# A sum of products moved from GpSimd to VectorE, with a PSUM copy of one operand and a buffer of its own

## The chip, the cores and the metric

The kernel runs on one core of one Trainium2 chip. The metric is device microseconds from the start to the end of one execution; the time before is the median of three runs. The engines are named as in the profile: PE is TensorE (matmul), PEld its loading of weights, DVE is VectorE, ACT is ScalarE, POOL is GpSimd, SP is SyncE, which issues most transfers.

## The reference

Two layers of a compressed interaction network, each followed by a batch norm over rows and embedding. The input has 4096 rows, 32 fields and 16 embedding values.

```python
def _cin_layer(out, x, W, b, gamma, beta):
    r, _, e = x.shape
    h = jnp.einsum('rne,rfe->rnfe', out, x).reshape(r, -1, e)
    h = jnp.einsum('rce,oc->roe', h, W) + b[None, :, None]
    return _batchnorm(h, gamma, beta)
h1 = _cin_layer(x, x, W1, b1, g1, beta1)
out, direct1 = (h1[:, :64], h1[:, 64:])
direct2 = _cin_layer(out, x, W2, b2, g2, beta2)
return jnp.concatenate([direct1, direct2], axis=1).sum(axis=-1)
```

W1 is 128 x 1024, W2 is 128 x 2048, all in 32-bit floats. Of the first layer 64 channels go on to the second, the other 64 to the output.

## The kernel before

The 65,536 sites (a row and an embedding value) stand along the free axis in tiles of 512. The **first pass** computes layer one for all of them, in 128 tiles; it is not touched by the change. Its kept channels go to memory, raw. The **second pass** computes layer two. Its loop runs over 64 **columns** c; a column is a pair of tiles, 512 sites of the one half of the rows and 512 of the other, and its matrix products are done in Strassen's way, in Winograd's form: seven products of half size in place of eight, with sums of operands made beforehand.

A column has four **stages**, k = 0 to 3, for the weight groups i = 3, 0, 1, 2 in that order. Stage 0 (i = `PLAIN`) is the **half stage**: one of its two blocks q is multiplied in the ordinary way, only q = 1 in Strassen's. Stages 1 to 3 are full. What a stage does, in the order of the code:

- ScalarE makes two factors, `f1` and `f2`: the kept channels, loaded as tile a, scaled and shifted by the batch norm. They lie in PSUM, in the pool `factors`, which has two banks.
- VectorE multiplies them with the inputs b and bx (L539): **M1**, `zz<-f,b`, makes B11 and B21, **M2**, `zz<-f,bx`, makes T3 and B22. All four stand in one tile z (named `zz`), as z[:, 0] = B11, z[:, 1] = T3, z[:, 2] = B22 and z[:, 3] = B21, each with its q; the pool of z has three tiles.
- GpSimd makes from z the **sum** T2 = T3 + B11 (L584) and the **differences** T1 = B22 - T2 and T4 = B21 - T2 in one instruction (L587), in a tile t. The pool of t has two tiles for the four stages of a column. The half stage uses one half of its tile.
- TensorE multiplies with weights of 64 output channels (L570), on one or the other half of its columns: in the half stage eight ordinary products, one of x1, two each of x32, x67 and x54; in a full stage two of x1 and four each of x32, x67 and x54. That is 15 + 3 x 14 = 57 products a column. x1 and x32 read z, x67 reads T2 and T3, x54 reads T1 and T4. The products of a stage go in the order x1, x32, then x54 of the stage before, then x67; after x67 of stage 3 stands x54 of stage 3 as well. The two halves take turns product by product, and since 57 is odd, the column that starts with the low half is followed by one that starts with the high half (`low_first`).

The sums of a column, four banks x11, x62, x34 and x57, are put together by `combine` during the next column, in steps that the main loop calls at fixed places: two copies of x11 by ScalarE, then an add by VectorE (tile `both`, stage 0), `e` = both + x62 ahead of M2 of stage 1, copies `u2` by ScalarE, `u3` behind M2 of stage 1, `e` from u3 ahead of M2 of stage 2, a reduction behind M1 of stage 3. `idle` gives some columns one more reduction, ahead of e.

Every engine runs its instructions in the order in which the code writes them: `queue` ties each to the one before on its engine.

```python
def queue(engine, make):
    with tc.issue_after(lasts[engine].ins) if engine in lasts else nullcontext():
        lasts[engine] = make()
    return lasts[engine]
```

Of the kernel before, what the change touches and what calls it, by code (L numbers as in the profile page):

```python
# [35 lines left out]
FP = mybir.dt.float32  # L36
AF = mybir.ActivationFunctionType
ALU = mybir.AluOpType
AX = mybir.AxisListType

P = 128
# [3 lines left out]
T = 512  # L45
# [16 lines left out]
def tile_cin(ctx: ExitStack, tc: tile.TileContext, xa, xb, xr, w1, w1m, w2, bn, out):  # L62
# [24 lines left out]
    class Stats:  # L87


        def __init__(self, name, tiles, groups=None):  # L90
            self.name = name
            full, rest = divmod(tiles - LAST, SG)
            self.sizes = [SG] * full + [rest] * (rest > 0) + [LAST]
            if groups is None:
                groups = const.tile([P, len(self.sizes), 3], FP, tag=f"groups{name}", name=f"groups{name}")
            self.groups = groups

            for g, size in enumerate(self.sizes):
                nc.vector.memset(groups[:, g, 0:1], size / LAST)
            self.group = self.at = 0  # L100
# [440 lines left out]
    def multiply_part(z, a, b, q):  # L541

        a = a.unsqueeze(1).to_broadcast([P, 2, T])
        dve(lambda: nc.vector.tensor_tensor(z[:, :, q], a, b.rearrange("p (k q) t -> p k q t", k=2)[:, :, q], ALU.mult))  # L544
# [10 lines left out]
    class Sums:  # L555
# [11 lines left out]
        def matmul(self, x, w, b, stop=False):  # L567
            start = x not in self.started
            self.started.add(x)
            queue("pe", lambda: nc.tensor.matmul(self.of[x], w, b, start=start, stop=stop))  # L570

    class Stage:


        def __init__(self, sums_, i, z, last):
            self.matmul, self.stop = sums_.matmul, last
            self.w = [weights(i, q) for q in range(2)]
            self.b11, self.t3, self.b22, self.b21 = (z[:, k] for k in range(4))
# [5 lines left out]
            queue("pool", lambda: nc.gpsimd.tensor_tensor(t[:, 0, q], z[:, 1, q], z[:, 0, q], ALU.add))  # L584

            twice = t[:, 0, q].unsqueeze(1).to_broadcast([P, 2, n, T])
            queue("pool", lambda: nc.gpsimd.tensor_tensor(t[:, 1:3, q], z[:, 2:4, q], twice, ALU.subtract))  # L587
# [5 lines left out]
        def ordinary(self, low_first, q):  # L593
            a11, a21, a12, a22, s1, s2, s3, s4 = self.w[q]
            minus_s3, minus_a21 = neg_sb[:, 0, q], neg_sb[:, 1, q]
            for x, u, y, v in ((3, s4, 2, a11), (5, s1, 4, a21)):
                self.two(low_first, (x, u, self.b22[:, q], False), (y, v, self.b11[:, q], False))
            for x, u, y, v in ((3, minus_s3, 2, a12), (5, minus_a21, 4, a22)):
                self.two(low_first, (x, u, self.t3[:, q], False), (y, v, self.b21[:, q], False))

        def x1(self, low_first):

            halves = [(x, self.w[q][0], self.b11[:, q], True) for x, q in zip((1, 0), self.qs)]
            if len(self.qs) == 1 and not low_first:
                halves[0] = (0, *halves[0][1:])
            self.two(low_first, *halves)

        def products(self, low_first, x, kx, bx, y, ky, by):
            for q in self.qs:
                stop = q == 1  # L610
                self.two(low_first, (x, self.w[q][kx], bx[:, q], stop), (y, self.w[q][ky], by[:, q], stop))

        def x32(self, low_first):
            self.products(low_first, 3, 7, self.b22, 2, 2, self.b21)
# [74 lines left out]
    for c in range(NC):  # L689
        raw, b, bx = loaded(c)  # L690
        sums_ = Sums()
        g = c // DIFF + 1
        if g < NC // DIFF:
            if c % DIFF == 2:
                with tc.issue_after(loads[-1].ins):
                    for k in range(2):
                        load_x(g, k)
            if c % DIFF == 4:
                for k in range(2):
                    queue("act", lambda: negate(k))  # L700
                idle += [lambda k=k: difference(k) for k in range(4)]
            if c % DIFF == 10:
                queue("act", lambda: store_difference(g))

        f1 = factor(raw[STAGES[0]], STAGES[0], 0)
        for k, i in enumerate(STAGES):

            z = z2pool.tile([P, 4, 2, T], FP, tag="zz", name="zz")
            if c == k == 0:

                f2 = factor(raw[i], i, 1)
                for q in range(2):
# [12 lines left out]
            if k == 1:  # L725
                step()
            if k < 3:
                f1 = factor(raw[STAGES[k + 1]], STAGES[k + 1], 0)
            if k == 0:
                step(2)  # L730
            if k == 2:

                step()
            for _ in range(min(len(sums_left), 4 if c == NC - 1 else 1)):
                queue("act", sums_left.pop(0))
            if k == 1:
                step()

            stage = Stage(sums_, i, z, k == 3)
# [111 lines left out]
```

## Time and profile before

| | |
|---|---|
| median of three runs | 2152.68 us (2151.9 to 2153.17) |
| the profiled execution | 2154.79 us, of which its span 2153.1 us |
| granted clock of TensorE, mean | 0.996 |
| GpSimd sum L584, full stage | 192 of 2372 ns |
| GpSimd differences L587, full stage | 192 of 4566 ns |
| GpSimd sum L584, half stage | 64 of 1288 ns |
| GpSimd differences L587, half stage | 64 of 2380 ns |
| VectorE M1 and M2 (L539) | 510 of 2.28 us |

The page counts busy time for each engine over the whole span; the first pass fills about the first 497 us and has nearly no work for GpSimd. A "wait" is idle time of an engine ahead of an instruction, put down to what ended it. The rows on which the argument rests stand in the prediction.

### The profile page before, as it was taken

What the parts mean: (1) busy time and instruction counts of PE and PEld (TensorE: products, weight loads), DVE (VectorE), ACT (ScalarE), POOL (GpSimd) and SP (SyncE); (2) the same over time, 40 slices, a digit from 0 to 9 for tenths busy, and PEclk for the clock granted to TensorE, in tenths of its full rate; (3) what the DMA queues carried; (4) which work ended last, traced back from release to release, by engine and by line L of the source; (5) the groups of instructions that cost most, each with busy time, mean ns of one, the idle gap of its engine ahead of it and who ended that gap; (6) DMA issues with size and microseconds to landing.
All of it is one profiled execution on the core that took longest, in us unless ns stands there. A gap on an engine that the chain in (4) does not pass through costs nothing.

```text
span 2153.1 us, 23463 instructions
## 1 busy us (share of the span) xinstructions
PE 2104.0 (98%) x8604; PEld 736.7 (34%) x8604; DVE 1846.4 (86%) x1317; ACT 969.0 (45%) x1522; POOL 1561.7 (73%) x519
## 2 busy tenths in 40 slices
PE   9999999999999999999999999999999999999996
PEld 3444444443333333333333333333333333333332
DVE  8898888988888888888888888888888888888885
ACT  3555555553444444444444444444444444444443
POOL 0000000006999999999999999999999999999996
PEclk9999999999999999999999999999999999999998
DMA  9999999997779777676787776676777777676751
GB/s 361 349 336 350 330 356 350 348 335 179 168 168 207 178 171 164 157 166 157 171 188 178 169 169 162 156 166 157 180 168 169 167 171 162 157 166 159 169 132 39
DMA packets 112019, 440.64 MB, mean 205 GB/s; under 512 B 13088, under 2 KB 13088, under 8 KB 103456
## 3 DMA queue, kind: packets, MB, share of 16 engines
q1 hardware_dynamic: 105456, 418.43, 73.4%
q10 hardware_dynamic: 6448, 20.72, 2.5%
q8 instruction: 67, 1.10, 0.2%
q14 instruction: 48, 0.39, 0.1%
HBM read 417.07 MB, written 22.02 MB: 204 GB/s over the span
## 4 chain that ended last, share of the span: by engine, by line
PE 44%; POOL 29%; DVE 14%; issue 12%; ACT 0%; DMA 0%; POOLq 0%; DVEq 0%; SPq 0%
PE x L570 22%; PE ps L384 21%; POOL t L587 20%; POOL t L584 9%; DVE zz L539 9%; DVE e L534 2%; DVE d L667 2%; PE ps L346 2%; ACT both L531 0%; DMA b<-in_xb 0%; DVE zz L544 0%; POOLq L847 0%; DVE xd L192 0%; PE running L412 0%; DVE u L534 0%
## 5 line engine op out<-in xcount | busy, mean ns | idle before, releaser
L587 POOL TENSOR_TENSOR t<-zz,t 128x2048 f32<-128x2048 f32 (+1 forms) x256 | 1029.0, 4020 | 20.1
L584 POOL TENSOR_TENSOR t<-zz 128x1024 f32<-128x1024 f32 (+1 forms) x256 | 537.8, 2101 | 545.1 <-DMA a<-h 493.0
L570 PE MATMUL x<-zz,s_sb 128*64 128x512 f32 x2048 | 920.4, 592 | 0.7 <-PE running L412 0.7
L570 PE MATMUL x<-zz,w_sb 128*64 128x512 f32 x2304 | 915.0, 592 | 0.0
L570 PE MATMUL x<-t,s_sb 128*64 128x512 f32 x1792 | 824.9, 594 | 12.1 <-POOL t L587 12.1
L531 ACT ACTIVATE f<-a,keep 128x512 f32<-128x512 f32 x512 | 398.0, 778 | 409.3 <-DVE zz L539 403.3
L539 DVE TENSOR_TENSOR zz<-f,b 128x2048 f32<-128x2048 f32 x255 | 581.0, 2279 | 0.0
L539 DVE TENSOR_TENSOR zz<-f,bx 128x2048 f32<-128x2048 f32 x255 | 580.6, 2277 | 0.0
L384 PE MATMUL ps<-z,w_sb 128*128 128x512 f32 x1024 | 449.9, 597 | 2.6 <-DVE z L353 2.6
L570 PE MATMUL x<-t,w_sb 128*64 128x512 f32 x896 | 429.6, 596 | 14.2 <-POOL t L587 14.1
L570 PEld LDWEIGHTS x<-zz,w_sb 128*64 128x64 f32 x2304 | 282.6, 137 | 347.2 <-issue 346.4
L570 PEld LDWEIGHTS x<-zz,s_sb 128*64 128x64 f32 x2048 | 272.2, 137 | 293.9 <-issue 289.8
L353 DVE TENSOR_TENSOR z<-a,b 128x2048 f32<-128x2048 f32 (+1 forms) x129 | 294.1, 2281 | 60.5 <-DMA b<-in_xb 36.6
L570 PEld LDWEIGHTS x<-t,s_sb 128*64 128x64 f32 x1792 | 239.9, 137 | 274.5 <-issue 224.1
L384 PEld LDWEIGHTS ps<-z,w_sb 128*128 128x128 f32 x1024 | 192.4, 190 | 257.9 <-issue 245.5
L534 DVE TENSOR_TENSOR both<-both,x 128x512 f32<-128x512 f32 x64 | 44.0, 688 | 183.2 <-ACT both L531 183.2
L310 ACT ACTIVATE e<-ps,bn_sb 128x512 f32<-128x512 f32 x127 | 87.3, 687 | 239.0 <-PE ps L384 224.0
L570 PEld LDWEIGHTS x<-t,w_sb 128*64 128x64 f32 x896 | 117.3, 137 | 154.7 <-issue 110.8
L531 ACT ACTIVATE u<-e,bn_sb 64x512 f32<-64x512 f32 x64 | 46.3, 723 | 223.9 <-DVE e L534 223.9
L531 ACT ACTIVATE both<-x 64x512 f32<-64x512 f32 x64 | 38.0, 594 | 189.4 <-PE x L570 189.4
L570 PE MATMUL x<-zz,neg_sb 128*64 128x512 f32 x256 | 120.3, 592 | 0.0
L485 ACT ACTIVATE unread<-e,center 128x512 f32<-128x512 f32 x124 | 89.6, 722 | 26.3 <-DVE e L534 24.5
(88 smaller groups left out, 884.6 us busy)
## 6 DMA issues: line engine op xcount, KB each, us to landing
a<-h SPq DMA_DIRECT2D x256, 512.0 KB, 5.3
a<-in_xa SPq DMA_DIRECT2D x128, 512.0 KB, 5.8
b<-in_xb SPq DMA_DIRECT2D x128, 512.0 KB, 6.8
b<-in_xb SPq DMA_DIRECT2D x64, 1024.0 KB, 8.0
bx<-in_xb SPq DMA_DIRECT2D x64, 512.0 KB, 7.0
bx<-x SPq DMA_DIRECT2D x64, 512.0 KB, 8.8
h<-kept ACTq DMA_DIRECT2D x64, 256.0 KB, 5.8
r<-in_xr SPq DMA_DIRECT2D x16, 512.0 KB, 8.0
```

Source lines behind the costliest of these rows:

```text
L310: nc.scalar.activation(e, ps, AF.Identity, bias=b1)
L346: nc.tensor.matmul(pss[t + k], w1_sb[rows, 4 + t % GROUP // 4, :], zr[rows, :], start=not ended, stop=ended)
L353: return nc.vector.tensor_tensor(z[:, k], a.rearrange("p (a t) -> p a t", a=2)[:, k].unsqueeze(2).to_broadcast([P, n, 2, T]), b.rearrange( ...
L384: nc.tensor.matmul(pss[t], w1_sb[:, m, :], z[:, m // 2, m % 2, :], start=(t == m == 0), stop=(t > 0 and m == 3))
L485: return nc.scalar.activation(unread, e[:, s], AF.Square, bias=center[:, s], accum_out=squares[:, s, c : c + 1])
L531: return queue("act", lambda: nc.scalar.activation(to, source, AF.Identity, **scale_bias))
L534: return dve(lambda: nc.vector.tensor_tensor(to, x, y, ALU.add))
L539: dve(lambda: nc.vector.tensor_tensor(z, a, b.rearrange("p (k q) t -> p k q t", k=2), ALU.mult))
L570: queue("pe", lambda: nc.tensor.matmul(self.of[x], w, b, start=start, stop=stop))
L584: queue("pool", lambda: nc.gpsimd.tensor_tensor(t[:, 0, q], z[:, 1, q], z[:, 0, q], ALU.add))
L587: queue("pool", lambda: nc.gpsimd.tensor_tensor(t[:, 1:3, q], z[:, 2:4, q], twice, ALU.subtract))
L667: lambda: nc.vector.tensor_reduce(d2[:, :, c, :], e.rearrange("p s (r e) -> p s r e", e=EMB), AX.X, ALU.add)
```

## The change

Three edits. The half stage's sum T2 is an add on VectorE (`sum_half`) instead of one on GpSimd. Its operand B11 comes from a copy that ScalarE writes to a bank of the pool `factors`, behind M1 of stage 0; its operand T3 comes from z. And the half stage's T2, T1 and T4 have a tile of their own, `th`, in a pool of one tile, so that the two tiles t serve the three full stages. GpSimd keeps the differences of the half stage.

```diff
+    hpool = ctx.enter_context(tc.tile_pool(name="hpool", bufs=1))
...
+    def sum_products(z):
+
+        t = tpool.tile([P, 3, 2, T], FP, tag="t", name="t")
+        queue("pool", lambda: nc.gpsimd.tensor_tensor(t[:, 0], z[:, 1], z[:, 0], ALU.add))
+
+        twice = t[:, 0].unsqueeze(1).to_broadcast([P, 2, 2, T])
+        queue("pool", lambda: nc.gpsimd.tensor_tensor(t[:, 1:3], z[:, 2:4], twice, ALU.subtract))
+        return t
+
+    def sum_half(z, b11):
+
+        t = hpool.tile([P, 3, 1, T], FP, tag="th", name="th")
+        add(t[:, 0, 0], z[:, 1, 1], b11)
+        twice = t[:, 0].to_broadcast([P, 2, T])
+        queue("pool", lambda: nc.gpsimd.tensor_tensor(t[:, 1:3, 0], z[:, 2:4, 1], twice, ALU.subtract))
+        return t
...
-        def __init__(self, sums_, i, z, last):
+        def __init__(self, sums_, i, z, last, t):
...
-            t = tpool.tile([P, 3, 2, T], FP, tag="t", name="t")
-            self.t2, self.t1, self.t4 = (t[:, k] for k in range(3))
-            q = slice(self.qs[0], 2)
-            n = len(self.qs)
-            queue("pool", lambda: nc.gpsimd.tensor_tensor(t[:, 0, q], z[:, 1, q], z[:, 0, q], ALU.add))
-
-            twice = t[:, 0, q].unsqueeze(1).to_broadcast([P, 2, n, T])
-            queue("pool", lambda: nc.gpsimd.tensor_tensor(t[:, 1:3, q], z[:, 2:4, q], twice, ALU.subtract))
+
+            self.t2, self.t1, self.t4 = ({q: t[:, k, q - self.qs[0]] for q in self.qs} for k in range(3))
...
                     multiply_part(z[:, 1:3], f2, bx, q)
+                b11 = factors.tile([P, T], FP, tag="f", name="b11")
+                act(b11, z[:, 0, 1])
             else:
                 multiply(z[:, 0::3], f1, b)
...
+                if i == PLAIN:
+                    b11 = factors.tile([P, T], FP, tag="f", name="b11")
+                    act(b11, z[:, 0, 1])
                 multiply(z[:, 1:3], f2, bx)
+            t = sum_half(z, b11) if i == PLAIN else sum_products(z)
```

The other lines of the diff follow the new form of `t` and z by q. The new lines shift the numbers: in the changed kernel the full stages' sum is L576, their differences L579, the half stage's differences L587, `add` L535, `multiply` L540, `act` L532.

On GpSimd, from the last stage of one column to the first full stage of the next (column 3; a number behind a name tells tiles apart, "waits" names the engines whose progress the instruction waits for), there stood:

```order
L584 TENSOR_TENSOR t_3170<-zz_3163 128x1024 [waits DVE_49,PE_49]
L587 TENSOR_TENSOR t_3170<-zz_3163,t_3170 128x2048 [waits Pool_49]
L584 TENSOR_TENSOR t_3221<-zz_3210 128x512 [waits DVE_49,PE_49]
L587 TENSOR_TENSOR t_3221<-zz_3210,t_3221 128x2x512 [waits Pool_49]
L584 TENSOR_TENSOR t_3253<-zz_3237 128x1024 [waits DVE_49,PE_49]
L587 TENSOR_TENSOR t_3253<-zz_3237,t_3253 128x2048 [waits Pool_49]
```

and stands now:

```order
L576 TENSOR_TENSOR t_3179<-zz_3172 128x1024 [waits DVE_49,PE_49]
L579 TENSOR_TENSOR t_3179<-zz_3172,t_3179 128x2048 [waits Pool_49]
L587 TENSOR_TENSOR th_3226<-zz_3219,th_3226 128x1024 [waits DVE_49]
L576 TENSOR_TENSOR t_3258<-zz_3248 128x1024 [waits DVE_49,PE_49]
L579 TENSOR_TENSOR t_3258<-zz_3248,t_3258 128x2048 [waits Pool_49]
```

The sum on 512 elements is gone, the differences of the half stage go to `th` and wait for VectorE, and the tiles t pass over the half stage.

On VectorE at the same place, from M2 of the last stage of one column to u3 in the next, there stood:

```order
L539 TENSOR_TENSOR zz_3163<-f_3167,bx_3055 128x2048
L539 TENSOR_TENSOR zz_3210<-f_3208,b_3191 128x2x1024
L539 TENSOR_TENSOR zz_3210<-f_3212,bx_3193 128x2048
L534 TENSOR_TENSOR both_3217<-both_3217,x11_3066 128x512
L539 TENSOR_TENSOR zz_3237<-f_3215,b_3191 128x2x1024
L534 TENSOR_TENSOR e_3239<-both_3217,x62_3067 128x512
L539 TENSOR_TENSOR zz_3237<-f_3241,bx_3193 128x2048
L534 TENSOR_TENSOR u3_3247<-u2_3243,x57_3069 128x512
```

and stands now:

```order
L540 TENSOR_TENSOR zz_3172<-f_3176,bx_3062 128x2048
L540 TENSOR_TENSOR zz_3219<-f_3217,b_3200 128x2x1024
L540 TENSOR_TENSOR zz_3219<-f_3221,bx_3202 128x2048
L535 TENSOR_TENSOR th_3226<-zz_3219,b11_3223 128x512
L535 TENSOR_TENSOR both_3231<-both_3231,x11_3073 128x512
L540 TENSOR_TENSOR zz_3248<-f_3229,b_3200 128x2x1024
L535 TENSOR_TENSOR e_3250<-both_3231,x62_3074 128x512
L540 TENSOR_TENSOR zz_3248<-f_3252,bx_3202 128x2048
```

The add `th<-zz,b11` has come in between M2 of the half stage and the add of `both`.

On ScalarE at the same place, from the factors of the half stage to u2, there stood:

```order
L531 ACTIVATE f_3208<-a_3196,keep_2781 128x512
L531 ACTIVATE f_3212<-a_3196,keep_2781 128x512
L531 ACTIVATE f_3215<-a_3198,keep_2781 128x512
L531 ACTIVATE both_3217<-x11_3066 64x512
L531 ACTIVATE both_3217<-x11_3066,bn_sb_201 64x512
L531 ACTIVATE f_3241<-a_3198,keep_2781 128x512
L531 ACTIVATE u2_3243<-e_3239,bn_sb_201 64x512
L531 ACTIVATE u2_3243<-e_3239,b2_swapped_2809 64x512
```

and stands now:

```order
L532 ACTIVATE f_3217<-a_3205,keep_2781 128x512
L532 ACTIVATE f_3221<-a_3205,keep_2781 128x512
L532 ACTIVATE b11_3223<-zz_3219 128x512
L532 ACTIVATE f_3229<-a_3207,keep_2781 128x512
L532 ACTIVATE both_3231<-x11_3073 64x512
L532 ACTIVATE both_3231<-x11_3073,bn_sb_201 64x512
L532 ACTIVATE f_3252<-a_3207,keep_2781 128x512
L532 ACTIVATE u2_3254<-e_3250,bn_sb_201 64x512
L532 ACTIVATE u2_3254<-e_3250,b2_swapped_2812 64x512
```

The copy `b11` has come in behind the second factor of the half stage. Since the pool has two banks that are taken in turn, the next factor (f_3215, now f_3229) takes the bank of that second factor; before, it took the bank of the first.

More of the change, by code (lines that the diff above doesn't have):

```diff
@@ L570, in matmul @@
             queue("pe", lambda: nc.tensor.matmul(self.of[x], w, b, start=start, stop=stop))
+    def sum_products(z):
[10 more added lines that the diff above has]
+        return t
     class Stage:
-        def __init__(self, sums_, i, z, last):
+        def __init__(self, sums_, i, z, last, t):
             self.matmul, self.stop = sums_.matmul, last
             self.w = [weights(i, q) for q in range(2)]
-            self.b11, self.t3, self.b22, self.b21 = (z[:, k] for k in range(4))
+            self.b11, self.t3, self.b22, self.b21 = ([z[:, k, q] for q in range(2)] for k in range(4))
             self.qs = (1,) if i == PLAIN else (0, 1)
-            t = tpool.tile([P, 3, 2, T], FP, tag="t", name="t")
-            self.t2, self.t1, self.t4 = (t[:, k] for k in range(3))
-            q = slice(self.qs[0], 2)
-            n = len(self.qs)
-            queue("pool", lambda: nc.gpsimd.tensor_tensor(t[:, 0, q], z[:, 1, q], z[:, 0, q], ALU.add))
-            twice = t[:, 0, q].unsqueeze(1).to_broadcast([P, 2, n, T])
-            queue("pool", lambda: nc.gpsimd.tensor_tensor(t[:, 1:3, q], z[:, 2:4, q], twice, ALU.subtract))
+            self.t2, self.t1, self.t4 = ({q: t[:, k, q - self.qs[0]] for q in self.qs} for k in range(3))
         def two(self, low_first, *halves):
@@ L596, in ordinary @@
             for x, u, y, v in ((3, s4, 2, a11), (5, s1, 4, a21)):
-                self.two(low_first, (x, u, self.b22[:, q], False), (y, v, self.b11[:, q], False))
+                self.two(low_first, (x, u, self.b22[q], False), (y, v, self.b11[q], False))
             for x, u, y, v in ((3, minus_s3, 2, a12), (5, minus_a21, 4, a22)):
-                self.two(low_first, (x, u, self.t3[:, q], False), (y, v, self.b21[:, q], False))
+                self.two(low_first, (x, u, self.t3[q], False), (y, v, self.b21[q], False))
         def x1(self, low_first):
-            halves = [(x, self.w[q][0], self.b11[:, q], True) for x, q in zip((1, 0), self.qs)]
+            halves = [(x, self.w[q][0], self.b11[q], True) for x, q in zip((1, 0), self.qs)]
             if len(self.qs) == 1 and not low_first:
@@ L610, in products @@
                 stop = q == 1
-                self.two(low_first, (x, self.w[q][kx], bx[:, q], stop), (y, self.w[q][ky], by[:, q], stop))
+                self.two(low_first, (x, self.w[q][kx], bx[q], stop), (y, self.w[q][ky], by[q], stop))
         def x32(self, low_first):
@@ L737, in tile_cin @@
                 step()
-            stage = Stage(sums_, i, z, k == 3)
+            stage = Stage(sums_, i, z, k == 3, t)
             low_first = c % 2 == 0
```

## The prediction

> **What bounds the kernel now.** I read the page first: busy shares, slices, the chain that ended last, one group. The rows of engines and slices give busy time and its tenths; a group row gives count, busy time, mean ns, idle time before it.
>
> ```profile
> PE 2104.0 (98%) x8604; PEld 736.7 (34%) x8604; DVE 1846.4 (86%) x1317; ACT 969.0 (45%) x1522; POOL 1561.7 (73%) x519
> ...
> POOL 0000000006999999999999999999999999999996
> ...
> PE 44%; POOL 29%; DVE 14%; issue 12%; ACT 0%; DMA 0%; POOLq 0%; DVEq 0%; SPq 0%
> ...
> L570 PE MATMUL x<-t,s_sb 128*64 128x512 f32 x1792 | 824.9, 594 | 12.1 <-POOL t L587 12.1
> ```
>
> GpSimd's 73% is an average over a first pass without it and a second pass where it is above 90%. The chain goes through TensorE, GpSimd and VectorE, so no engine alone sets the time. The group has 1792/64 = 28 records a column, for 14 products in the code: a product is two records. A second-pass stretch, by the view of windows (PE, PEld, DVE, ACT, POOL busy, granted clock, DMA share, GB/s):
>
> ```profile
> 1000.00:1200.00 200.00, 197.01 (x896) 64.54 (x894) 173.61 (x115) 87.22 (x135) 191.77 (x64) 1.00 0.75 173
> ```
>
> GpSimd works 191.77 of 200 us and still waits, TensorE likewise, by the waits (us, times, longest):
>
> ```profile
> PEld x L570 <- POOL t L587: 93.1, 97, 3.6
> ...
> DVE both L534 <- ACT both L531: 183.2, 64, 5.9
> ...
> POOL t L584 <- PE x L570: 51.7, 63, 0.9
> ...
> DVE e L534 <- PE x L570: 29.2, 33, 2.3
> ```
>
> GpSimd waits for TensorE once in 63 of 64 columns, and TensorE for GpSimd. That is a loop; the timeline shows it (start, duration, [idle <- releaser]):
>
> ```profile
> 1190.43 1.30 POOL L584 TENSOR_TENSOR t<-zz 128x512 f32<-128x512 f32 x1
> ...
> 1202.00 2.38 POOL L584 TENSOR_TENSOR t<-zz 128x1024 f32<-128x1024 f32 x1 [0.82 <-PE x L570]
> 1204.46 4.56 POOL L587 TENSOR_TENSOR t<-zz,t 128x2048 f32<-128x2048 f32 x1
> 1208.98 2.35 POOL L584 TENSOR_TENSOR t<-zz 128x1024 f32<-128x1024 f32 x1
> 1211.41 4.55 POOL L587 TENSOR_TENSOR t<-zz,t 128x2048 f32<-128x2048 f32 x1
> 1215.92 1.28 POOL L584 TENSOR_TENSOR t<-zz 128x512 f32<-128x512 f32 x1
> 1217.28 2.37 POOL L587 TENSOR_TENSOR t<-zz,t 128x1024 f32<-128x1024 f32 x1
> ...
> 1227.47 2.37 POOL L584 TENSOR_TENSOR t<-zz 128x1024 f32<-128x1024 f32 x1 [0.82 <-PE x L570]
> ```
>
> ```profile
> 1189.16 1.02 PE L570 MATMUL x<-t,s_sb 128*64 128x512 f32 x2
> 1190.54 0.64 PE L570 MATMUL x<-t,w_sb 128*64 128x512 f32 x1 [0.36 <-POOL t L587]
> ...
> 1201.32 0.59 PE L570 MATMUL x<-t,w_sb 128*64 128x512 f32 x1
> ...
> 1207.33 0.59 PE L570 MATMUL x<-t,w_sb 128*64 128x512 f32 x1
> ...
> 1213.77 0.59 PE L570 MATMUL x<-zz,s_sb 128*64 128x512 f32 x1
> ...
> 1214.63 1.02 PE L570 MATMUL x<-zz,s_sb 128*64 128x512 f32 x2
> 1216.01 0.64 PE L570 MATMUL x<-t,s_sb 128*64 128x512 f32 x1 [0.37 <-POOL t L587]
> ```
>
> A column lasts 1215.92 - 1190.43 = 25.49 us, by 1202.00 and 1227.47 it is 25.47: I take 25.48. **The loop**: T2 of stage 2 starts at 1202.00, when x54 of stage 0 has freed its buffer (last record 1201.32 + 0.59 = 1201.91, a lag of 0.09). GpSimd runs back to back until 1211.41 + 4.55 = 1215.96; 0.05 later, at 1216.01, TensorE gets x54 of stage 3, and 11.46 after that, at 1227.47, the next buffer is free. 13.96 + 0.05 + 11.46 = 25.47.
>
> **TensorE's floor**: from 1207.33 to 1213.77 lie 15 record steps, 0.4293 each, two records side by side on the two column halves. So 57 products of a column take 57 x 0.4293 = 24.47 us. The loop costs 25.48 - 24.47 = 1.01 us a column.
>
> **The change part by part.** *Removed from GpSimd*: the half stage's sum, 1217.28 - 1215.92 = 1.36 us a column start to start. The row has 1.28 us as the duration. (The Trainium skill, "Perfetto Trace Analysis", section "GPSIMD Engine Instruction", says to time GpSimd by start-to-start spacing and not by reported durations; the two rows agree that the two differ, by 0.08. By durations, 2.35 + 4.55 for sum and differences, loop A below would be 0.08 shorter, 24.42 us, and the floor of 24.47 would set those columns.) Alone this removal would buy nothing: T2 of stage 2 starts when x54 of stage 0 frees its buffer, however early GpSimd is there.
>
> *The own buffer* breaks that wait. The two tiles t now serve three stages, so T2 of stage 2 waits for x54 of stage 3 of the column before, long done. Late next are two loops.
>
> **Loop A, the buffer again**: T2 of stage 3 now takes the tile of stage 1 and waits for its x54, whose last record ends at 1207.33 + 0.59 = 1207.92. With the lag, 1208.01; sum and differences take 1215.96 - 1208.98 = 6.98; TensorE starts 0.05 later, at 1215.04, where an unstalled TensorE would take it at 1214.63 (the records there run without a partner). It is 0.41 late, but only once: after that the two column halves run staggered by as much, and the half due for the next x54 comes free that much later anyway. What counts is the loop's length. x54 of stage 3 to the end of x54 of stage 1 is 1207.92 - 1190.54 = 17.38, and 0.09 + 6.98 + 0.05 + 17.38 = **24.50 us**.
>
> **Loop B, VectorE's e**:
>
> ```profile
> 1190.22 0.69 DVE L534 TENSOR_TENSOR e<-both,x 128x512 f32<-128x512 f32 x1 [0.94 <-PE x L570]
> 1190.83 2.28 DVE L539 TENSOR_TENSOR zz<-f,bx 128x2048 f32<-128x2048 f32 x1
> ...
> 1204.74 2.27 DVE L539 TENSOR_TENSOR zz<-f,b 128x2048 f32<-128x2048 f32 x1
> 1206.94 2.27 DVE L539 TENSOR_TENSOR zz<-f,bx 128x2048 f32<-128x2048 f32 x1
> 1211.86 0.69 DVE L534 TENSOR_TENSOR both<-both,x 128x512 f32<-128x512 f32 x1 [2.64 <-ACT both L531]
> 1212.46 2.28 DVE L539 TENSOR_TENSOR zz<-f,b 128x2048 f32<-128x2048 f32 x1
> ...
> 1218.05 0.69 DVE L534 TENSOR_TENSOR u<-u,x 128x512 f32<-128x512 f32 x1 [0.32 <-PE x L570]
> ...
> 1231.97 2.27 DVE L539 TENSOR_TENSOR zz<-f,bx 128x2048 f32<-128x2048 f32 x1
> ```
>
> In every second column (the order of the halves alternates) e waits for the last product of x67 of stage 3, begun at 1189.16; M2 of stage 1 stands behind e and ends at 1190.83 + 2.28 = 1193.11. Then GpSimd does three full stages, 3 x 6.98 (also 1208.98 - 1202.00), with lags of 0.09 and 0.05, to the next x54 of stage 3: 3.95 + 0.09 + 20.94 + 0.05 = 25.03 us from that product. x54 itself started 0.41 after that product (loop A), so the column lasts 25.03 - 0.41 = **24.62**. The other columns have loop A's 24.50. Mean 24.56.
>
> *Added on ScalarE*: the copy of B11, between f2 of stage 0 and f1 of stage 1. The trace has no such copy; the nearest row is a factor (SBUF to PSUM, 128x512), 0.78. *Added on VectorE*: T2 behind M2 of stage 0. Nearest row: both, 0.69, with 0.60 to the next start; the far end is GpSimd's 1.36 for the same work. I take 0.60. `both` and M1 of stage 1 are queued behind it, and GpSimd's differences of stage 0 wait for it.
>
> ```profile
> 1207.05 0.78 ACT L531 ACTIVATE f<-a,keep 128x512 f32<-128x512 f32 x1 [1.42 <-DVE zz L539]
> ...
> 1210.53 0.59 ACT L531 ACTIVATE both<-x 64x512 f32<-64x512 f32 x1 [2.70 <-PE x L570]
> ```
>
> Cover: VectorE stands idle 2.64 us ahead of `both` (183.2/64 = 2.86 in the mean). In the places of this column the copy runs from 1207.05 to 1207.83 beside M2, T2 from 1209.14 (M2's start and the 2.20 from M1 to M2) to 1209.83. The copy takes a factor bank, so f1 of stage 1 must wait for M2's end (1206.94 + 2.27 = 1209.21) and ends at 1210.03, still 0.50 ahead of the ScalarE `both` at 1210.53. VectorE's own loop: from `both` to M2's end is 1231.97 + 2.27 - 1211.86 = 22.38, of which the 0.32 of u goes with the earlier x54; then f1 0.04 + 0.78 and the ScalarE part of `both`, 1211.86 - 1210.53 + 0.01 = 1.34: 24.22, under 24.47. T2, at 0.60 or at 1.36, fits beside f1 and that part (2.16). So I cost both additions at nothing; without that cover T2 would cost 0.60 x 63 = 38 us.
>
> *First column*, where VectorE feeds GpSimd:
>
> ```profile
> 501.44 1.22 DVE L544 TENSOR_TENSOR zz<-f,bx 128x1024 f32<-128x1024 f32 x1
> 502.57 2.28 DVE L539 TENSOR_TENSOR zz<-f,b 128x2048 f32<-128x2048 f32 x1
> ...
> 507.13 2.37 POOL L584 TENSOR_TENSOR t<-zz 128x1024 f32<-128x1024 f32 x1 [0.44 <-DVE zz L539]
> ...
> 523.50 4.52 POOL L587 TENSOR_TENSOR t<-zz,t 128x2048 f32<-128x2048 f32 x1
> ```
>
> f1 of stage 1 must now wait for the last part of M2, 501.44 + 1.22 = 502.66; with 0.04 + 0.78 + 0.04 M1 of stage 1 starts at 503.52 instead of 502.57. GpSimd waits for VectorE at 507.13 and then has no gap up to 523.50 + 4.52 = 528.02, so this column's x54 comes 0.95 later.
>
> **Sum.** 63 column intervals x (25.48 - 24.56) = 58.0; less 0.95: 57.0 us. The profiled execution took 2154.79 us (span 2153.1 and 1.7 around it), 2.1 above the median 2152.68: 2097.8 against it, **2095.7** against the median.
>
> **The rivals.**
>
> *VectorE sets every column.* Loop B uncredited is 25.03. If e waited for the last product in all columns, or the stagger gave nothing back, the gain would be 63 x 0.45 - 0.95 = 27.4: 2125 us. Against it: e waits for TensorE in 33 columns of 64 and not in all, and the lateness of one column is covered by the stagger in the next. Chance 0.10.
>
> *The change does not do what it says*: if T2 of stage 3 waited as long as T2 of stage 2 does, the time would stay, 2152.7. The order of instructions puts sum and differences of the half stage outside the tiles t, and loop A is 0.98 shorter, so only an unseen wait could do it: 0.03.
>
> *Slower: the new add waits for GpSimd.* Its place, 1209.14, lies beside GpSimd's sum of stage 3 (1208.98 to 1211.33), and in a quicker column beside the differences, 4.55. If VectorE could not read z while GpSimd reads, the add would be held up to 4.55, and `both` and M1 with it: 22.06 + 0.60 + 4.55 = 27.21 a column, (27.21 - 25.48) x 63 + 0.95 = 110 us more, 2263. It decides from a wait of 25.48 - 22.66 = 2.82 us.
>
> ```profile
> L534 DVE TENSOR_TENSOR both<-both,x 128x512 f32<-128x512 f32 x64 | 44.0, 688 | 183.2 <-ACT both L531 183.2
> ```
>
> Against it: 64 such adds, one input from SBUF and one from PSUM as the new one, take 688 ns in the mean, beside a GpSimd that is busy nearly always. (The Trainium skill, "SBUF — State Buffer", section "Who interferes with whom", says that a VectorE instruction with two SBUF inputs contends with a GpSimd instruction that reads SBUF, and one with at most one SBUF input does not. By that rule the add from the PSUM copy is free of it; the 688 ns agree. No run here shows an add with both inputs in SBUF beside GpSimd.) Chance 0.04.
>
> **How the numbers follow.** The forecast has 0.83. Its bounds: TensorE's floor and a first column at no cost, 63 x 1.01 = 63.6, 2089.1, or 2088 with the 0.8 us by which the fastest run lies under the median; and loop B not absorbed in every second column, (24.50 + 25.03)/2 = 24.77, 63 x 0.71 - 0.95 = 43.8, 2108.9. Twelve second-pass columns also have a reduction ahead of e, which I put at the 0.60 of VectorE's other 512-element steps; in the half of them where e has no slack that is up to 3.6 us: 2112. So 2088 to 2112, which leaves out the 0.17 of the other cases. A measurement tells 0.2%, 4.3 us, from no change. Faster: 0.83 and 0.10, 0.93; the same 0.03; slower 0.04.
>
> **What the profile after would show.** Successive half-stage differences on GpSimd 24.5 to 24.6 us apart, in turn longer and shorter; sums of stage 2 without a wait for TensorE, those of stage 3 with none or a few tenths; the wait of `both` down from 2.9 us to 1 to 2; the new add near 0.69 us and the copy near 0.78, neither waited for by GpSimd; TensorE's gap at x54 of stage 3 gone from about 1 us to a tenth. Wrong would be: columns of 25.0 with e waiting each time (first rival), a wait at x54 as before (second), an add of over 0.8 us or GpSimd waiting for it (third); GpSimd durations that grow when VectorE moves nearer; a granted clock under the 1.00 of the windows, where TensorE would lose more than all of this.

## The result and the profile after

The changed kernel takes 2099.96 us (median of 4 runs, 2099.49 to 2101.45), the kernel before, run beside it, 2152.93 us (4 runs, 2151.9 to 2156.91): a ratio of 0.9752, 95% interval 0.9735 to 0.9769. That is 53.0 us faster. The forecast was 2095.7 us, 57.0 us faster, with a range of 2088 to 2112. The profiled execution took 2099.52 us, its span is 2097.7 us.

From the page of the kernel after, the same rows as of before: busy engines, the slices of GpSimd, the chain that ended last. Behind them is the 200-us window of the second pass.

```profile
PE 2073.1 (99%) x8604; PEld 1037.5 (49%) x8604; DVE 1885.7 (90%) x1381; ACT 1007.1 (48%) x1586; POOL 1479.1 (71%) x455
...
POOL 0000000003999999999999999999999999999995
...
PE 94%; DVE 2%; DMA 2%; POOL 1%; issue 0%; ACT 0%; SPq 0%; DVEq 0%; POOLq 0%; ACTq 0%
```

```profile
1000.00:1200.00 200.00, 200.00 (x930) 108.10 (x928) 185.79 (x127) 95.34 (x148) 188.08 (x58) 1.00 0.77 178
```

GpSimd went from 519 instructions to 455 and VectorE from 1317 to 1381: the 64 sums of the half stage have moved. The chain, which was 44% TensorE and 29% GpSimd, is 94% TensorE. In the window TensorE starts 930 records where it started 896: in pairs at 0.4293 us they fill 199.6 us of the 200, where they filled 192.3.

The column is measured from one half-stage difference on GpSimd to another. These are the timeline's rows of the first, the third and the last (64th), of the kernel before; then the same of the kernel after, with two columns in between.

```profile
504.31 2.37 POOL L587 TENSOR_TENSOR t<-zz,t 128x1024 f32<-128x1024 f32 x1
...
554.85 2.38 POOL L587 TENSOR_TENSOR t<-zz,t 128x1024 f32<-128x1024 f32 x1
...
2109.11 2.38 POOL L587 TENSOR_TENSOR t<-zz,t 128x1024 f32<-128x1024 f32 x1
```

```profile
501.49 2.37 POOL L587 TENSOR_TENSOR th<-zz,th 128x1024 f32<-128x1024 f32 x1 [493.26 <-DVE th L535]
...
553.03 2.38 POOL L587 TENSOR_TENSOR th<-zz,th 128x1024 f32<-128x1024 f32 x1
...
1192.54 2.37 POOL L587 TENSOR_TENSOR th<-zz,th 128x1024 f32<-128x1024 f32 x1
1195.67 2.38 POOL L576 TENSOR_TENSOR t<-zz 128x1024 f32<-128x1024 f32 x1 [0.76 <-DVE zz L540]
...
1202.66 2.37 POOL L576 TENSOR_TENSOR t<-zz 128x1024 f32<-128x1024 f32 x1
...
1210.09 2.37 POOL L576 TENSOR_TENSOR t<-zz 128x1024 f32<-128x1024 f32 x1 [0.43 <-PE x L571]
...
1217.06 2.36 POOL L587 TENSOR_TENSOR th<-zz,th 128x1024 f32<-128x1024 f32 x1
1220.81 2.37 POOL L576 TENSOR_TENSOR t<-zz 128x1024 f32<-128x1024 f32 x1 [1.38 <-DVE zz L540]
...
1241.69 2.38 POOL L587 TENSOR_TENSOR th<-zz,th 128x1024 f32<-128x1024 f32 x1
...
2052.98 2.37 POOL L587 TENSOR_TENSOR th<-zz,th 128x1024 f32<-128x1024 f32 x1
```

Before, 61 columns took 1554.26 us, 25.480 each; after, 1499.95 us, 24.589 each. Two neighbours differ: 1217.06 - 1192.54 = 24.52 and 1241.69 - 1217.06 = 24.63. The sum of stage 2 (1202.66) no longer waits for TensorE; that of stage 3 (1210.09) does, here by 0.43, and in 26 columns of 64 by the waits below; that of stage 1 waits for VectorE's M2, by 0.76 and 1.38 in turn. The waits of the kernel after, over all columns (us in total, times, longest):

```profile
DVE both L535 <- ACT both L532: 95.6, 64, 4.9
...
POOL t L576 <- DVE zz L540: 72.3, 64, 2.1
...
PEld x L571 <- POOL t L579: 28.7, 67, 3.6
DVE e L535 <- PE x L571: 26.2, 26, 2.7
...
POOL t L576 <- PE x L571: 13.3, 26, 2.1
```

**Where the time came from.** 61 columns gained 0.890 us each, 54.3 us. The two intervals ahead of the third difference took 50.54 and take 51.54, 1.0 us lost. That leaves 53.3 between the first and the last difference, and 53.0 between the medians. (The profiled executions lie 55.3 apart: before the second pass, which the change doesn't touch, and at its end they differ by the other 2 us, and the one of before was 2.1 above its median.)

### The profile page after: what moved, and what is told of

Same layout as the page of the kernel before. It is cut to its first block, busy times and chain, and to the rows that moved or that the text cites. A ratio compares the mean times of both kernels' runs of the same rounds, so it can differ in the third digit from the quotient of the medians.

```text
span 2097.7 us, 23531 instructions
## 1 busy us (share of the span) xinstructions
PE 2073.1 (99%) x8604; PEld 1037.5 (49%) x8604; DVE 1885.7 (90%) x1381; ACT 1007.1 (48%) x1586; POOL 1479.1 (71%) x455
## 4 chain that ended last, share of the span: by engine, by line
PE 94%; DVE 2%; DMA 2%; POOL 1%; issue 0%; ACT 0%; SPq 0%; DVEq 0%; POOLq 0%; ACTq 0%
PE x L571 74%; PE ps L384 19%; PE ps L346 1%; DMA b<-in_xb 1%; DVE z L353 1%; POOL t L579 1%; DMA a<-in_xa 1%; POOL t L576 0%; DVE zz L545 0%; DVE zz L540 0%; PE running L412 0%; DVE stats L106 0%; DVE e L535 0%; DVE d L801 0%; ACT f L532 0%
## 5 line engine op out<-in xcount | busy, mean ns | idle before, releaser
L571 PE MATMUL x<-zz,s_sb 128*64 128x512 f32 x2048 | 947.2, 592 | 1.0 <-PE running L412 0.7
L571 PE MATMUL x<-zz,w_sb 128*64 128x512 f32 x2304 | 886.9, 593 | 0.0
L579 POOL TENSOR_TENSOR t<-zz,t 128x2048 f32<-128x2048 f32 x192 | 875.5, 4560 | 15.1
L571 PE MATMUL x<-t,s_sb 128*64 128x512 f32 x1536 | 699.5, 595 | 0.0
L532 ACT ACTIVATE f<-a,keep 128x512 f32<-128x512 f32 x512 | 398.0, 778 | 418.1 <-DVE zz L540 360.6
L540 DVE TENSOR_TENSOR zz<-f,b 128x2048 f32<-128x2048 f32 x255 | 580.6, 2277 | 0.1
L540 DVE TENSOR_TENSOR zz<-f,bx 128x2048 f32<-128x2048 f32 x255 | 579.9, 2274 | 0.0
L576 POOL TENSOR_TENSOR t<-zz 128x1024 f32<-128x1024 f32 x192 | 455.5, 2373 | 85.7 <-DVE zz L540 72.3
L587 POOL TENSOR_TENSOR th<-zz,th 128x1024 f32<-128x1024 f32 x64 | 152.0, 2375 | 493.3 <-DVE th L535 493.3
L571 PEld LDWEIGHTS x<-zz,w_sb 128*64 128x64 f32 x2304 | 306.3, 137 | 162.2 <-issue 70.1
L571 PE MATMUL x<-t,w_sb 128*64 128x512 f32 x768 | 364.2, 597 | 2.8 <-POOL t L579 2.7
L571 PEld LDWEIGHTS x<-t,s_sb 128*64 128x64 f32 x1536 | 207.5, 137 | 226.2 <-issue 180.0
L532 ACT ACTIVATE u<-e,bn_sb 64x512 f32<-64x512 f32 x64 | 46.2, 722 | 218.3 <-DVE e L535 218.3
L571 PE MATMUL x<-th,s_sb 128*64 128x512 f32 x256 | 130.8, 592 | 0.0
L535 DVE TENSOR_TENSOR both<-both,x 128x512 f32<-128x512 f32 x64 | 44.0, 688 | 95.6 <-ACT both L532 95.6
```

Source lines behind the costliest of these rows:

```text
L532: return queue("act", lambda: nc.scalar.activation(to, source, AF.Identity, **scale_bias))
L535: return dve(lambda: nc.vector.tensor_tensor(to, x, y, ALU.add))
L540: dve(lambda: nc.vector.tensor_tensor(z, a, b.rearrange("p (k q) t -> p k q t", k=2), ALU.mult))
L576: queue("pool", lambda: nc.gpsimd.tensor_tensor(t[:, 0], z[:, 1], z[:, 0], ALU.add))
L579: queue("pool", lambda: nc.gpsimd.tensor_tensor(t[:, 1:3], z[:, 2:4], twice, ALU.subtract))
L587: queue("pool", lambda: nc.gpsimd.tensor_tensor(t[:, 1:3, 0], z[:, 2:4, 1], twice, ALU.subtract))
```

## The experiments

The theory to test: the wait for a free tile t was the bound, so the tile of its own gives the gain and the move to VectorE gives none by itself; behind it stand loop A (the tile again, stage 1 to stage 3) and loop B (VectorE's `e`), 0.03 and 0.15 over TensorE's floor of 24.47. The rivals: the gain comes from the work that GpSimd no longer does; or VectorE sets the pace. All edits are against the changed kernel. "Column" is the mean of the 61 columns from the third to the last half-stage difference in the profile, as above. All ratios are to the kernel before, which ran beside them (medians 2152.9 to 2154.5). Some rows come from different chips, so a small difference between two rows rests on the columns as much as on the times.

| kernel | us, median (range) | ratio, 95% interval | column, us |
|---|---|---|---|
| the change, first | 2099.96 (2099.49-2101.45) | 0.9752 (0.9735-0.9769) | 24.589 |
| the change, again | 2099.08 (2098.65-2099.79) | 0.9742 (0.9726-0.9758) | 24.586 |
| own buffer only | 2098.61 (2096.27-2100.27) | 0.9743 (0.9729-0.9758) | 24.595 |
| move only | 2161.45 (2161.12-2163.63) | 1.0039 (1.0024-1.0053) | 25.587 |
| both from SBUF | 2115.12 (2113.28-2115.8) | 0.9819 (0.9805-0.9834) | 24.838 |
| x67 first | 2092.84 (2092.05-2094.74) | 0.9719 (0.9704-0.9733) | 24.510 |
| tiles apart | 2098.77 (2096.51-2098.89) | 0.9742 (0.9726-0.9758) | 24.617 |
| x67 first, tiles apart | 2090.37 (2089.6-2091.25) | 0.9707 (0.9692-0.9721) | 24.471 |
| the same, sum on GpSimd | 2096.43 (2095.59-2099.15) | 0.9733 (0.9718-0.9747) | 24.587 |
| the add four times | 2112.86 (2110.74-2114.42) | 0.981 (0.9796-0.9825) | 24.779 |
| the add six times | 2203.31 (2202.51-2224.77) | 1.0255 (1.0208-1.0301) | 26.210 |

### The own buffer without the move

```diff
-        add(t[:, 0, 0], z[:, 1, 1], b11)
+        queue("pool", lambda: nc.gpsimd.tensor_tensor(t[:, 0, 0], z[:, 1, 1], z[:, 0, 1], ALU.add))
...
-                    b11 = factors.tile([P, T], FP, tag="f", name="b11")
-                    act(b11, z[:, 0, 1])
```

> The half stage keeps its sum on GpSimd, without the copy of B11, but has the tile of its own. Theory 1 (the wait for the buffer of t closed the loop, and the own buffer is what broke it): GpSimd's work sets the column, 3 x 6.98 + 1.36 + 2.34 = 24.64 us, TensorE's floor being 24.47; so 24.64 to 24.75 a column and 2100 to 2107 us, and the changed kernel's move of the sum is worth 0 to 7 us of the 53. Theory 2 (the gain came from the load taken off GpSimd, 1.36 us a column): the column stays near 25.4, 2145 to 2153 us.

2098.61 us, a little under the 2100 to 2107 expected: the whole gain, without the move. The timeline of GpSimd in this kernel shows what holds the column now.

```profile
1213.52 1.29 POOL L585 TENSOR_TENSOR th<-zz 128x512 f32<-128x512 f32 x1
1214.89 2.38 POOL L587 TENSOR_TENSOR th<-zz,th 128x1024 f32<-128x1024 f32 x1
1217.26 2.38 POOL L576 TENSOR_TENSOR t<-zz 128x1024 f32<-128x1024 f32 x1
...
1224.23 2.40 POOL L576 TENSOR_TENSOR t<-zz 128x1024 f32<-128x1024 f32 x1
...
1231.23 2.36 POOL L576 TENSOR_TENSOR t<-zz 128x1024 f32<-128x1024 f32 x1
...
1238.17 1.28 POOL L585 TENSOR_TENSOR th<-zz 128x512 f32<-128x512 f32 x1
```

No row has a wait, and in this kernel's list of waits GpSimd has only 0.7 us behind its first instruction of the second pass: it works back to back, and its own work, 1238.17 - 1213.52 = 24.65 us, is the column. So the sum on GpSimd is not free here, it is the bound; but the changed kernel has another bound of almost the same length. That the two agree to 0.01 us in the mean is chance; the pair of experiments with both loops gone, below, takes them apart.

### The move without the own buffer

```diff
-        t = hpool.tile([P, 3, 1, T], FP, tag="th", name="th")
+        t = tpool.tile([P, 3, 2, T], FP, tag="t", name="t")[:, :, 0:1]
```

> The half stage's sum goes to VectorE with the copy of B11, but its tile comes from the two tiles t as before the change. Theory 1: the loop from x54 of stage 0 through stage 2's sum on GpSimd to x54 of stage 3 is untouched, 25.48 us a column, 2150 to 2157 us; besides, VectorE's add now waits for x54 of stage 2 of the column before, some 3 us after the place it had, with the add of both behind it. Theory 2 (the load): 2096 to 2110 us, as the changed kernel.

2161.45 us, above the 2150 to 2157 expected: slower than before by 0.4%, interval 0.24 to 0.53%. The rows are from this kernel's waits, and from its timeline of VectorE and of GpSimd.

```profile
DVE t L534 <- PE x L570: 192.0, 62, 3.9
...
POOL t L575 <- DVE zz L539: 144.8, 63, 2.9
```

```profile
1217.53 0.69 DVE L534 TENSOR_TENSOR t<-zz,b 128x512 f32<-128x512 f32 x1 [3.16 <-PE x L570]
1218.13 0.68 DVE L534 TENSOR_TENSOR both<-both,x 128x512 f32<-128x512 f32 x1
1218.73 2.28 DVE L539 TENSOR_TENSOR zz<-f,b 128x2048 f32<-128x2048 f32 x1
...
1221.53 2.28 DVE L539 TENSOR_TENSOR zz<-f,bx 128x2048 f32<-128x2048 f32 x1
```

```profile
1223.98 2.38 POOL L575 TENSOR_TENSOR t<-zz 128x1024 f32<-128x1024 f32 x1 [2.25 <-DVE zz L539]
```

The sum of stage 2 on GpSimd no longer waits for TensorE, so the loop of before is not what holds this kernel. Another wait for a tile t has taken its place: the add, now early on VectorE, takes the tile of stage 2 of the column before and waits 192.0/62 = 3.1 us for TensorE to be done with it. `both`, M1, `e` and M2 of stage 1 are queued behind it, and GpSimd, with 1.36 us less to do, waits 2.3 us a column for that M2. This and the experiment before show that the gain is the buffer's; a wait on an engine is priced by what is queued behind it there.

### No copy: both operands from SBUF

```diff
-        add(t[:, 0, 0], z[:, 1, 1], b11)
+        add(t[:, 0, 0], z[:, 1, 1], z[:, 0, 1])
...
-                    b11 = factors.tile([P, T], FP, tag="f", name="b11")
-                    act(b11, z[:, 0, 1])
```

> The changed kernel without the copy of B11: VectorE's add reads T3 and B11 both from z in SBUF, and f1 of stage 1 has its old bank again. If VectorE's second input from SBUF does not meet GpSimd's reads: an add of 0.69 us, the column at 24.59 or a little less, 2096 to 2101 us. If it does and waits for the GpSimd instruction that runs (the sum of stage 3, 1210.09 to 1212.46, where the add stood at 1211.72): an add that ends up to 0.8 us later, under the 1.4 to 1.5 us that VectorE is idle ahead of both, so still 2100 to 2103 us, but a longer add in the trace. If it waits for the sum and the differences behind it (4.57 us more): both comes some 3 us late in each column, VectorE's loop is about 27 us, 2240 to 2265 us. If GpSimd is held instead: its instructions beside the add grow by up to 0.7 us, 24.6 to 25.2 a column, 2100 to 2140 us. By the Trainium skill, SBUF - State Buffer, section Who interferes with whom, the one that issues second waits for the first.

15 us slower than the change. The first two rows are the group of the half stage's add in the changed kernel and in this one; then this kernel's timeline of GpSimd and of VectorE.

```profile
L535 DVE TENSOR_TENSOR th<-zz,b 128x512 f32<-128x512 f32 x64 | 44.0, 687 | 6.7
```

```profile
L535 DVE TENSOR_TENSOR th<-zz 128x512 f32<-128x512 f32 x64 | 90.3, 1411 | 2.2
```

```profile
1216.85 2.34 POOL L576 TENSOR_TENSOR t<-zz 128x1024 f32<-128x1024 f32 x1 [0.96 <-PE x L571]
1219.27 4.87 POOL L579 TENSOR_TENSOR t<-zz,t 128x2048 f32<-128x2048 f32 x1
```

```profile
1217.91 1.83 DVE L535 TENSOR_TENSOR th<-zz 128x512 f32<-128x512 f32 x1
1220.70 0.69 DVE L535 TENSOR_TENSOR both<-both,x 128x512 f32<-128x512 f32 x1 [0.95 <-ACT both L532]
```

The mean add takes 1411 ns instead of 687. In the rows it starts at 1217.91 inside GpSimd's sum, which ends at 1219.19, and ends at 1219.74, 0.55 after it; the differences behind the sum then take 4.87 us instead of 4.56. All 62 adds that begin inside such a sum end 0.54 to 0.56 us after it, however long they had stood, and the differences of stage 3 take 4.87 us in the mean instead of 4.55, those of the other stages as before. So the add waits for the running GpSimd instruction, and the next one, beside which the add then runs, is longer by 0.32. Two cases of the expectation came together, the waiting add and the held GpSimd. The differences of stage 3 lie in both loops, and 0.32 is near to what the column lost: it went from 24.589 to 24.838, and (24.838 - 24.589) x 62 = 15.4 us is the whole loss. This is what the copy in PSUM is worth here. (The Trainium skill, "SBUF — State Buffer", section "Who interferes with whom", says that a VectorE instruction with two SBUF inputs contends with a GpSimd instruction that reads SBUF and one with at most one SBUF input doesn't; the 1411 and the 687 ns agree with both halves of it.)

### Loop B: x67 of stage 3 ahead of x54 of stage 2

```diff
+            if k == 3:
+                stage.x67(not low_first)
...
-            stage.x67(not low_first)
+            if k < 3:
+                stage.x67(not low_first)
```

> The changed kernel with one order changed: in stage 3 x67 stands ahead of x54 of stage 2. So x62 is complete four products (1.72 us) earlier, and VectorE's e (0.94 us of waiting in every second column) should not wait. If loop B sets the longer columns: they fall from 24.66 to loop A's 24.52, the mean from 24.589 to 24.52, 4 us less, 2093 to 2097 us. If loop A or GpSimd alone sets them: no change there. In the first column TensorE's one gap of 3.27 us ahead of the last x54 becomes two shorter ones, one ahead of x67 (sum of stage 3) and one ahead of x54; if the gap's length is what lowered the granted clock to 0.57 behind it, the clock stays at 1.00 there and 1.5 us more are gained.

`e` gets its last product earlier. 2092.84 us, just under the 2093 to 2097 expected, and 24.510 a column. This kernel's waits:

```profile
POOL t L576 <- PE x L571: 44.6, 62, 1.2
...
DVE e L535 <- PE x L571: 0.9, 1, 0.9
```

VectorE's `e` now waits for TensorE once in all, 0.9 us, where it waited 26 times; every column is alike, and in 62 of 64 the sum of stage 3 waits for its tile. That is loop A alone, reckoned at 24.50. Of the 7.1 us against the change, 61 x 0.079 = 4.8 are the columns'. Another 1.7 us lie ahead of the third half-stage difference, where the granted clock of TensorE now stays at 1.00; the last section comes back to that.

### Loop A: the tile of the sum apart from that of the differences

```diff
-        t = tpool.tile([P, 3, 2, T], FP, tag="t", name="t")
+        t2 = tpool.tile([P, 2, T], FP, tag="t2", name="t2")
...
+        t14 = tpool.tile([P, 2, 2, T], FP, tag="t14", name="t14")
```

> The changed kernel with the full stages' T2 in two tiles of its own and T1 and T4 in two others, in the same space. The sum of stage 3 then waits for x67 of stage 1 only, and only its differences for x54 of stage 1: loop A shrinks from 24.50 to 17.38 + 0.09 + 4.55 + 0.05 = 22.07 us. If GpSimd's wait for the buffer (13.3 us in 26 waits) is all that is between the short columns, 24.52, and TensorE's floor of 24.47: 3 us less at most, 2096 to 2100 us, since loop B still sets every second column and the stagger of the halves already covers most of it. If loop A set both kinds of columns: 24.47 in all, 2092 us.

The sum waits for no product now, as its own tile comes free earlier. 2098.77 us: no change, the interval is that of the change run again. By the half-stage differences the two kinds of columns are 24.21 and 25.04 in the mean, where they were 24.52 and 24.66: what the one gained the other gave back. By the first record of x54 of stage 3 on TensorE they are 24.53 and 24.65, with the edit and without. So loop A alone costs nothing while loop B is there: two columns in a row have the same length together. Why the long columns give back just that much (the stagger of the halves, by the prediction's argument) was not tested apart.

### Both loops, with the sum on VectorE and on GpSimd

> x67 ahead of x54 in stage 3 and the split tiles together. With loops A and B both gone, TensorE's floor sets the column: 24.47 against 24.51 with the first alone, 2.5 us less than it, 2088 to 2092 us. If something else holds x67_first at 24.51: no difference from 2092.8.

> x67 ahead of x54 in stage 3 and the split tiles, but the half stage's sum on GpSimd in its own tile, without the copy. GpSimd's own work, 3 x 6.98 + 1.36 + 2.34 = 24.64 (measured 24.60 a column with the own buffer alone), is then the longest thing, above TensorE's floor of 24.465. If so: 24.60 a column, 62 x 0.13 = 8 us over x67_first_split, less what the first column gains without the copy (1 us): 2096 to 2099 us, and the move of the sum is worth 7 us once the other loops are gone. If the move is worth nothing even then: 2089 to 2092 us.

Both have the edits of the last two experiments; the second also has that of the own buffer without the move. The window of the second pass, for the one and then for the other:

```profile
1000.00:1200.00 200.00, 200.00 (x934) 80.99 (x932) 186.47 (x127) 94.79 (x148) 189.58 (x59) 1.00 0.78 179
```

```profile
1000.00:1200.00 200.00, 200.00 (x930) 116.72 (x928) 179.96 (x118) 90.52 (x141) 197.49 (x65) 1.00 0.77 179
```

With the sum on VectorE the column is 24.471, TensorE's floor as reckoned (57 x 0.4293 = 24.47), and 2090.37 us the best time here: 9.6 us under the changed kernel as first run, 8.7 under it as run again. With the sum on GpSimd, which is then busy 197.49 of 200 us, it stays at 24.587, 2096.43 us. So with both loops gone the move does buy something, 61 x 0.116 = 7.1 us in the columns, less the 1.0 us that the copy costs in the first: 6.1 us in all, as between the medians. With both loops in place it bought nothing; with one of them gone it was not tried.

### The cover of the add: four and six times

```diff
-        add(t[:, 0, 0], z[:, 1, 1], b11)
+        for _ in range(4):
+            add(t[:, 0, 0], z[:, 1, 1], b11)
```

(six in the second of the two)

> The changed kernel with VectorE's new add done four times over, to test that it costs nothing. 3 x 0.60 = 1.8 us more a column, of which VectorE's idle time ahead of both (95.6 us / 64 = 1.49) takes most: its loop is 22.06 + 0.10 + 4 x 0.605 = 24.58, as long as the column now. If the cover is as reckoned: 2100 to 2108 us. If the add stands on the path: 1.8 us x 63 = 113 us more, 2213.

> The same with the add six times over: VectorE's loop is 22.06 + 0.10 + 6 x 0.605 = 25.79 us, 1.2 above the column now, so the cover is gone: 62 x 1.20 = 74 us more, 2170 to 2180 us. If VectorE's loop is shorter than reckoned, less by 62 us for each us.

Both came out longer than expected. These are rows of VectorE's timeline, of the kernel with four and of that with six:

```profile
1218.50 2.85 DVE L535 TENSOR_TENSOR th<-zz,b 128x512 f32<-128x512 f32 x4
1221.27 0.68 DVE L535 TENSOR_TENSOR both<-both,x 128x512 f32<-128x512 f32 x1
...
1243.15 2.85 DVE L535 TENSOR_TENSOR th<-zz,b 128x512 f32<-128x512 f32 x4
```

```profile
1308.12 4.29 DVE L535 TENSOR_TENSOR th<-zz,b 128x512 f32<-128x512 f32 x6
1312.33 0.68 DVE L535 TENSOR_TENSOR both<-both,x 128x512 f32<-128x512 f32 x1
```

Adds to the same tile follow each other by (2.85 - 0.69)/3 = 0.72 us, not by the 0.60 between a single one and its neighbour: `both` starts 2.77 and 4.21 us after the first add. In both kernels `both` has no cover left (of its 64 waits for ScalarE one remains), so VectorE's loop is the column. Most columns last 24.65 and 26.09 us; the twelve with a reduction ahead of `e` last 25.26 and 26.70, and the means are 24.78 and 26.21. So VectorE's loop without the adds is 24.65 - 2.77 = 21.88, by the other kernel 26.09 - 4.21 = 21.88. The prediction has 22.06 (24.22 less the cover of 2.16), 0.18 too long; that there is a cover, and that it ends between one add and four, is shown. What made the two kernels slower than expected is the spacing, and the twelve columns, which the expectation left out. (The profiled execution of six adds is the longest of its four: its first pass, which no edit touches, took 21 us more; the columns are all in the second. The median of 2203.31 lies 103.4 above the change, 62 x (26.21 - 24.59) = 100.4.)

### The change again

> The changed kernel once more, on the chip and in the rounds of the run beside it. The column 24.59 again. The first column tells whether the drop of the granted clock behind TensorE's gap of 3.27 us is fixed or varies: so far gaps of 3.22 to 3.28 us at this place were followed by a clock of about 0.6 in four profiles (the changed kernel, two_sbuf, split_t, add_x6) and by 1.00 in four (before, own_buffer_only, move_only, add_x4). If it varies from execution to execution, a first column of 30.3 to 30.4 us may show; if it belongs to the kernel, 31.8 again.

2099.08 us, 24.586 a column: as at first. In the first column the granted clock drops here too, to 0.65.

## Why the prediction was right, step by step

- **The removal from GpSimd alone buys nothing, the own buffer breaks the loop.** Shown from both sides: the buffer alone gives the whole gain, the move alone none (0.4% slower). In the move alone the wait of stage 2's sum, which the prediction gives as the reason, is replaced by another, so the run shows the outcome but doesn't test that reason by itself.
- **Loop A, 24.50.** Shown: 24.510 where it is the only loop.
- **Loop B, 24.62 in every second column.** Shown: moving x67 took the waits of `e` away and 0.08 us a column. Columns of 24.50 and 24.62 were forecast, 24.52 and 24.66 are there; the mean is 24.59, not 24.56. The lags of both loops were read from single rows; the 0.03 by which their sum is short is worth 61 x 0.03 = 1.8 us.
- **The floor, 24.47.** Shown: 24.471 with both loops gone.
- **Both additions at nothing.** The add takes 687 ns as reckoned, and `both` still waits 95.6/64 = 1.49 us for ScalarE, so there is cover to spare; the copy, bounded by a factor of 0.78, takes 602 ns. VectorE's own loop is 21.88 without the add, so with it 22.48, about 2.1 under the column. Four adds already cost 13 us, 12 x (25.26 - 24.59) = 8 of them in the columns with a reduction ahead of `e`.

```profile
L532 ACT ACTIVATE b<-zz 128x512 f32<-128x512 f32 x64 | 38.5, 602 | 92.1 <-DVE zz L540 89.1 <-issue 3.0
```

- **The first column, 0.95 later: where the sum fell short.** From the first x product to x54 of stage 3 it took 528.08 - 500.49 = 27.59 before and takes 526.92 - 498.32 = 28.60 now, 1.01 more: the term itself was right. But then comes a slow stretch that the sum did not have. The rows are TensorE's timeline of the kernel before, then of the kernel after, and the window of the 3.4 us from 527.0 of the kernel after.

```profile
500.49 0.61 PE L570 MATMUL x<-zz,s_sb 128*64 128x512 f32 x1 [0.74 <-PE running L412]
...
528.08 0.64 PE L570 MATMUL x<-t,w_sb 128*64 128x512 f32 x1 [2.67 <-POOL t L587]
```

```profile
498.32 0.61 PE L571 MATMUL x<-zz,s_sb 128*64 128x512 f32 x1 [0.74 <-PE running L412]
...
523.22 1.02 PE L571 MATMUL x<-t,s_sb 128*64 128x512 f32 x2
526.92 0.87 PE L571 MATMUL x<-t,w_sb 128*64 128x512 f32 x1 [2.68 <-POOL t L579]
...
527.58 1.06 PE L571 MATMUL x<-t,w_sb 128*64 128x512 f32 x1
...
530.81 0.59 PE L571 MATMUL x<-zz,w_sb 128*64 128x512 f32 x1
```

```profile
527.00:530.40 3.40, 3.40 (x10) 1.09 (x12) 0.50 (x1) 0.46 (x1) 3.40 (x2) 0.53 0.27 63
```

From 526.92 to 530.81 lie five record steps, 3.89 us where 5 x 0.4293 are 2.15: the granted clock in the window is 0.53 (0.54 in the last section's table, where the window starts at 526.92), and 1.74 us are lost. So the first column lost 2.7 us, not 0.95. With the 0.03 a column that is 1.8 + 1.7 = 3.5 of the 4.0 by which the gain fell short; the rest is within what two executions differ by. Both profiled executions of the changed kernel have the slow stretch; whether the others have it no profile shows. The two misses point the same way, so neither hid the other.

- **The rivals.** VectorE as the bound of every column: no, `e` waits in 26 columns. No effect: no. The add held up by GpSimd: not from PSUM, and from SBUF at a price of 15 us, far below the 110 reckoned for a wait of a whole 4.55 us instruction in all columns, since the add began inside the shorter sum and waited only for the rest of it.

## What to carry to other kernels

Where two busy engines wait for each other in every round, reckon the loop, not the load: the time is the sum of the work and the lags from one freeing of the buffer to the next, and taking work off an engine shortens it only where that work lies in the loop. Ask of each buffer which stage's release the next user waits for; a tile apart for the one small stage was worth 55 us here, and moving its work without the tile cost 8, as it set up a new wait on an engine with more queued behind it. After the first loop is broken, work out the next two before another edit, since removing only one of a pair that alternates may change nothing in the mean (tiles apart: no change by itself, 2.5 us once loop B is gone).

## What the runs showed of the hardware

The slow stretch in the first column is a matter of TensorE's granted clock. Nine of the profiles have the same gap in the first column ahead of x54 of stage 3, some 2.7 us idle by the row of that record. The granted clock in the 3.4 us behind it:

| kernel | gap by the row, us | clock behind it |
|---|---|---|
| before | 2.67 | 1.00 |
| own buffer only | 2.67 | 1.00 |
| move only | 2.68 | 1.00 |
| four adds | 2.69 | 1.00 |
| the change | 2.68 | 0.54 |
| the change, again | 2.69 | 0.65 |
| both from SBUF | 2.67 | 0.65 |
| tiles apart | 2.67 | 0.67 |
| six adds | 2.61 | 0.56 |
| the three with x67 first | 2.18 to 2.19, then 0.96 to 0.99 | 1.00 |

The same gap was followed by the slow clock in five profiles and not in four, among them kernels with the same code at this place (the change and the one with four adds differ only on VectorE). Where x67 filled it in part none of three profiles has the slow clock, too few to tell that from chance. What decides among the nine is open: the gap falls at another point of each execution, and no run here moved it on purpose. (The Trainium skill, "TensorE: Matmul & The Clock Gate", section "Part 1: The HAM clock gate (the "warmup" mystery)", has the clock judged in free-running windows of about 3.4 us, which would let the place of the gap in the window decide; but it asks for an idle window, and the gaps here are shorter than one.)

Left open too: a third tile t, which would remove loop A in another way, was not tried.
